# Products of zeros on TensorE during the first load, a different load order, and alternating half groups at the end of a two-layer graph network kernel

## The chip, the cores and the metric

The kernel runs on one NeuronCore of a Trainium2 chip. The metric is the device time of one execution in microseconds (us). TensorE (PE in the profile) multiplies matrices and writes to PSUM; its weight loads (PEld) have a row of their own. VectorE (DVE), ScalarE (ACT) and GpSimd (POOL) do elementwise work and reductions, and SyncE (SP), ACT and POOL issue the DMA transfers.

## The reference

The input x is (16, 1024, 64): 16 batches, 1024 nodes, 64 channels; adj is 1024 x 1024. Two layers follow each other, each with a residual and a layer norm over the channels. Cut to what is computed:

```python
# layer 0
Q, K, V = x @ Wq.T + bq, x @ Wk.T + bk, x @ Wv.T
score = softmax(einsum('bnc,bmc->bnm', Q, K), axis=1)
out   = einsum('bnm,bmc->bnc', score @ adj, V)
x = layernorm(x + out)
# layer 1: both supports are adj
x1 = adj @ x;  x2 = 2 * (adj @ x1) - x
x_cat = [x, x1, x2, x1', x2']      # the second support again, from x and x1
x = layernorm(x + x_cat @ weight + bias)
```

All of it is float32.

## The kernel before, in words

**Layout.** Two batches make a pair, so that a pair's 2 x 64 channels fill the 128 partitions; there are eight pairs (`NP = 8`). The 1024 nodes are eight blocks of 128 (`K8 = 8`). `xs` holds x with the nodes on the partitions, `xT` holds it with the channels on the partitions, and `aT` holds the transposed adj.

**Algebra.** A term that is constant along the softmax axis drops out, so `bq` is not used and the scores are x times `GY`, with `GY = m_w^T xT + gb`. Here `m_w` is the product of the two score weights and `gb` that of one weight with `bk`. Layer 0 forms `U = adj @ x` once, and applies `Wv` after the sum.

**The start (lines 65 to 136).** `wq` and `wk` are 128 x 128 tiles that VectorE sets to zero and whose two diagonal 64 x 64 blocks are loaded: `wq`, `wk` and `bkp` in turn for each half, six transfers in ACT's queue. SP loads x in eight transfers of 512 KB and then aT in eight of 512 KB. GpSimd issues five transfers of weights that are used later, and builds the identity `ident` after them (`make_identity`, lines 84 and 85). `transposed(p)` turns the eight blocks of a pair on TensorE against `ident` into a PSUM tile `pt` (line 104), and ACT copies it to `xT` (line 105). `score_weight` turns `wq` and `wk` (lines 109, 110), VectorE copies them to `wn` (line 111), and `score_weight_2` forms `m_w` and `gb` (lines 115 to 118). `project(p)` makes `GY` of a pair with two products (line 126), and VectorE adds `gb` on the way out of PSUM (line 127). The order is written out by hand:

```python
transposed(0); pm = score_weight(); transposed(1); score_weight_2(pm)
for p in range(NP):
    if p + 2 < NP: transposed(p + 2)
    project(p)
```

PSUM has a pool `ps` of three tiles for all of these, and a pool `pacc` with one tile, `acc`.

**Order of work.** The scheduler is manual: each engine executes in the order in which the program names its instructions. In the profile, one float32 product of 128 columns or more appears as two matmul records; a transpose appears as one.

**Products with adj (`product`).** A 1024 x 1024 product with adj is done by one level of a Strassen-like scheme with seven block products, `p1` to `p7`, instead of eight. `step(name, g, rows)` accumulates one block product of a group `g` (two row blocks of 128 rows; `rows` picks one of them: a half group) into a PSUM tile that a chain of steps shares, in 16 products (8 for a half group), all on line 267. After each step VectorE or ACT takes the state of the tile to the result: line 283 adds it to what is there, line 287 adds it to another tensor. The next step of the same chain accumulates into the same tile, so it waits until that has been read. `p4` is in chain "a", `p3` in chain "b".

**Middle.** For each of 64 (pair, node block) steps the scores are formed, exponentiated and multiplied with `U`; then come the norm of layer 0 and the weights of layer 1. Then there are two more products with adj.

**The end (lines 499 to 543).** `leave(i, c, g, skip, blocks)` is the last layer norm of a group: ACT squares (line 507) and VectorE sums. For a whole group GpSimd takes the inverse root and multiplies. For a half group (`blocks == 1`) it is ACT's square root and VectorE's reciprocal and product (lines 171 to 179 and 513), so that VectorE has four operations, an addition, a sum, a reciprocal and a product, with two of ACT between them. Each block is stored by a transfer of SP. The last four lines of the order are

```python
for g in range(2):
    step("p4", g); leave(1, 0, g)
for i in range(2):
    step("p3", 1, (i,)); leave(0, 1, 1, i, 1)
```

Of the kernel before, what the change touches and what calls it, by code (L numbers as in the profile page):

```python
# [9 lines left out]
FP = mybir.dt.float32  # L10
# [8 lines left out]
def gnn_kernel(  # L19
# [13 lines left out]
    nc = tc.nc  # L33
    ctx.enter_context(tc.manual_schedule())
    N, B, C = out.shape
    P = 128
    K8 = N // P
    NP = B // 2
# [6 lines left out]
    const = ctx.enter_context(tc.tile_pool(name="const", bufs=1))  # L45
# [3 lines left out]
    pacc = ctx.enter_context(tc.tile_pool(name="pacc", bufs=1, space=bass.MemoryType.PSUM))  # L49

    def ps_tile(name):
        return ps.tile([P, 2 * H], FP, tag="ps", name=name)


    xs = big.tile([P, NP, K8, P], FP, tag="xs", name="xs")
    aT = big.tile([P, K8, N], FP, tag="aT", name="aT")
    x_in = x.rearrange("p q k b c -> p q k (b c)")
    a_in = adjT.rearrange("(k p) i -> p k i", p=P)

    def pair_weight(name):  # L60
        w = const.tile([P, P], FP, tag=name, name=name)
        nc.vector.memset(w, 0.0)
        return w

    wq, wk = pair_weight("wq"), pair_weight("wk")
    bkp = const.tile([P, 1], FP, tag="bkp", name="bkp")
    raw = const.tile([P, 5, C], FP, tag="raw", name="raw")
    w1s = const.tile([P, 5, C], FP, tag="w1s", name="w1s")
    for j in range(2):
        s = slice(j * C, (j + 1) * C)  # L70
        nc.scalar.dma_start(wq[s, s], wqT)
        nc.scalar.dma_start(wk[s, s], wkT)
        nc.scalar.dma_start(bkp[s], bk[:, None])
    for p in range(NP):
        nc.sync.dma_start(xs[:, p], x_in[:, p])
    for k in (4, 5, 6, 7, 0, 1, 2, 3):
        nc.sync.dma_start(aT[:, k], a_in[:, k])
    for j in range(2):
        s = slice(j * C, (j + 1) * C)
        nc.gpsimd.dma_start(w1s[s], w1.rearrange("(s c) o -> c s o", c=C))  # L80
        nc.gpsimd.dma_start(raw[s, 3], wvT)
    nc.gpsimd.dma_start(raw[:, 4], b1[None, :].to_broadcast([P, C]))

    ident = const.tile([P, P], FP, tag="ident", name="ident")
    make_identity(nc, ident)
    expo = const.tile([P, G], FP, tag="expo", name="expo")
    nc.vector.memset(expo, -0.5)
    eps = const.tile([P, 1], FP, tag="eps", name="eps")
# [11 lines left out]
    def transposed(p):  # L100

        pt = ps_tile("pt")
        for k in range(K8):
            nc.tensor.transpose(pt[:, ts(k, P)], xs[:, p, k, :], ident)  # L104
        nc.scalar.activation(xT[:, p], pt, AF.Copy)  # L105

    def score_weight():
        pw = ps_tile("pw")
        nc.tensor.transpose(pw[:, 0:P], wq, ident)
        nc.tensor.transpose(pw[:, P : 2 * P], wk, ident)  # L110
        nc.vector.tensor_copy(wn, pw[:, 0 : 2 * P].rearrange("p (a o) -> p a o", a=2))
        return pw

    def score_weight_2(pm):
        nc.tensor.matmul(pm[:, H : H + P], wn[:, 1], wn[:, 0], start=True, stop=True)
        nc.tensor.matmul(pm[:, 2 * H - P : 2 * H - P + 1], wn[:, 0], bkp, start=True, stop=True)
        nc.vector.tensor_copy(m_w, pm[:, H : H + P])
        nc.vector.tensor_copy(gb, pm[:, 2 * H - P : 2 * H - P + 1])
# [4 lines left out]
    def project(p):  # L123
        pg = ps_tile("pg")
        for h in range(2):
            nc.tensor.matmul(pg[:, ts(h, H)], m_w, xT[:, p, ts(h, H)], start=True, stop=True)
        nc.vector.tensor_scalar(GY[:, p], pg, gb, None, op0=ALU.add)

    transposed(0)
    pm = score_weight()  # L130
    transposed(1)
    score_weight_2(pm)
    for p in range(NP):
        if p + 2 < NP:
            transposed(p + 2)
        project(p)


# [17 lines left out]
    for j in range(2):  # L156
        s = slice(j * C, (j + 1) * C)
        nc.vector.tensor_copy(wv[s, s], raw[s, 3])

    def row_sums(sq, g=G):  # L160
        var = small.tile([P, g], FP, tag="var", name="var")
        nc.vector.tensor_reduce(var, sq, AX.X, ALU.add)  # L162
        nc.vector.tensor_scalar(var, var, 1.0 / C, EPS, op0=ALU.mult, op1=ALU.add)  # L163
        return var

    def inverse_root(var, g=G):
        rstd = small.tile([P, g], FP, tag="rstd", name="rstd")
        nc.gpsimd.tensor_tensor(rstd, var, expo[:, 0:g], ALU.pow)  # L168
        return rstd[:, :, None].to_broadcast([P, g, C])

    def inverse_root_2(sq, g):


        var = small.tile([P, g], FP, tag="var", name="var")
        nc.vector.tensor_reduce(var, sq, AX.X, ALU.add)  # L175
        rstd = small.tile([P, g], FP, tag="rstd", name="rstd")
        nc.scalar.activation(rstd, var, AF.Sqrt, bias=eps, scale=1.0 / C)  # L177
        nc.vector.reciprocal(rstd, rstd)
        return rstd[:, :, None].to_broadcast([P, g, C])
# [27 lines left out]
    def by_pair(t):  # L207

        return t.rearrange("p k (q f) -> p q k f", q=NP)
# [190 lines left out]
    step, sums = product(S, xs, by_pair(U), acc_group=1)  # L400
# [53 lines left out]
    def blocked(t):  # L454
        return t.rearrange("p q (k f) -> p q k f", k=K8)

    p = NP - 1
# [4 lines left out]
    step, sums = product(S, blocked(GY), by_pair(Z), xs)  # L462
# [36 lines left out]
    def leave(i, c, g, skip=0, blocks=2):  # L499

        first_block = i * HB + 2 * g + skip
        r = R[:, first_block : first_block + blocks, ts(c, H)].rearrange(
            "p i (b c) -> p i b c", c=C
        )
        nb = B // 2
        sq = att.tile([P, blocks, nb, C], FP, tag="rT", name="sq2")
        nc.scalar.activation(sq, r, AF.Square)  # L507
        rows = sq.rearrange("p i b c -> p (i b) c")
        if blocks == 1:
            engine, rstd = nc.vector, inverse_root_2(rows, nb)  # L510
        else:
            engine, rstd = nc.gpsimd, inverse_root(row_sums(rows))
        engine.tensor_tensor(  # L513
            r, r, rstd.rearrange("p (i b) c -> p i b c", i=blocks), ALU.mult
        )
        for n in range(blocks):
            nc.sync.dma_start(out[ts(first_block + n, P), ts(c, nb)], r[:, n])

    step, sums = product(S, by_pair(Z), by_pair(R), blocked(xT))
# [15 lines left out]
    for g in range(2):  # L535
        step("p7", g)
        leave(1, 1, g)
    for g in range(2):
        step("p4", g)
        leave(1, 0, g)  # L540
    for i in range(2):
        step("p3", 1, (i,))
        leave(0, 1, 1, i, 1)


# [38 lines left out]
```

## Time and profile before

| | |
|---|---|
| time, median of 3 runs | 623.25 us (622.73 to 623.89) |
| profiled execution, span | 621.4 us |
| TensorE matmul busy | 606.1 us, 98% of the span |
| VectorE busy | 335.3 us, 54% |
| ScalarE busy | 225.2 us, 36% |
| GpSimd busy | 86.5 us, 14% |
| DMA | 14.30 MB, mostly in the first 25 us |

TensorE is busy from about 5 us after the start to about 7 us before the end. A row of groups gives the busy time, the mean duration of one instruction, the idle time before them, and what ended most of that. In a timeline, a line is the start in us, the length of the merged stretch in us, the engine, the line of code, the operation, and what ended the idle time before it. Matmul ends are modelled, so that distances between starts say more than lengths[...].

### The profile page before, as it was taken

What the parts mean: (1) busy time and instruction counts of PE and PEld (TensorE: products, weight loads), DVE (VectorE), ACT (ScalarE), POOL (GpSimd) and SP (SyncE); (2) the same over time, 40 slices, a digit from 0 to 9 for tenths busy, and PEclk for the clock granted to TensorE, in tenths of its full rate; (3) what the DMA queues carried; (4) which work ended last, traced back from release to release, by engine and by line L of the source; (5) the groups of instructions that cost most, each with busy time, mean ns of one, the idle gap of its engine ahead of it and who ended that gap; (6) DMA issues with size and microseconds to landing.
All of it is one profiled execution on the core that took longest, in us unless ns stands there. A gap on an engine that the chain in (4) does not pass through costs nothing. (4 is left out here: it accounts for less than half of the span.)

```text
span 621.4 us, 5758 instructions
## 1 busy us (share of the span) xinstructions
PE 606.1 (98%) x2246; PEld 263.1 (42%) x2246; DVE 335.3 (54%) x554; ACT 225.2 (36%) x376; POOL 86.5 (14%) x47
## 2 busy tenths in 40 slices
PE   5999999999999999999999999999999999999994
PEld 4544444433334444343434434344444444444441
DVE  0498212157786767768686776735462332234434
ACT  2300100056656667676666767651100000000011
POOL 2000004400030200303030020300000000140374
PEclk9999999999999999999999999999999999999998
DMA  9600000200000000000000000000000000010012
GB/s 296 264 0 0 1 0 0 68 1 0 2 0 1 1 1 2 1 0 2 0 1 2 0 2 1 0 1 0 1 0 0 1 0 0 1 69 0 34 69 101
DMA packets 5835, 14.30 MB, mean 23 GB/s; under 512 B 1088, under 2 KB 1152, under 8 KB 5808
## 3 DMA queue, kind: packets, MB, share of 16 engines
q1 hardware_dynamic: 5136, 13.63, 5.9%
q0 software_dynamic: 192, 0.23, 0.2%
q8 instruction: 18, 0.29, 0.2%
q10 hardware_dynamic: 480, 0.07, 0.1%
q14 instruction: 9, 0.07, 0.0%
HBM read 9.73 MB, written 4.19 MB: 22 GB/s over the span
## 5 line engine op out<-in xcount | busy, mean ns | idle before, releaser
L313 DVE TENSOR_SCALAR_CACHE_REDUCE e<-sc 128x1024 f32<-128x1024 f32 x128 | 151.6, 1222 | 68.1 <-PE sc L306 68.1
L320 ACT ACTIVATE e<-e,nm 128x1024 f32<-128x1024 f32 x128 | 146.2, 1143 | 74.6 <-DVE e L313 74.5
L306 PE MATMUL sc<-xT,GY 64*128 64x512 f32 x512 | 128.1, 615 | 0.5 <-DVE e L313 0.5
L343 PE MATMUL acc<-e,us 128*64 128x512 f32 x512 | 124.0, 605 | 0.3 <-DVE us L331 0.3
L168 POOL TENSOR_TENSOR rstd<-var,expo 128x16 f32<-128x16 f32 x14 | 40.6, 2903 | 423.5 <-DVE var L163 423.5
L306 PEld LDWEIGHTS sc<-xT,GY 64*128 64x128 f32 x512 | 44.6, 186 | 73.5 <-issue 49.9
L507 ACT ACTIVATE sq<-GY 128x1024 f32<-128x1024 f32 (+1 forms) x9 | 8.7, 962 | 163.1 <-DVE GY L283 151.5
L267 PE MATMUL p<-T,S 128*128 128x512 f32 x144 | 62.8, 592 | 0.0
L343 PEld LDWEIGHTS acc<-e,us 128*64 128x64 f32 x512 | 31.0, 136 | 71.0 <-issue 62.9
L267 PEld LDWEIGHTS p<-T,S 128*128 128x128 f32 x144 | 27.4, 190 | 34.4 <-issue 34.4
L285 ACT ACTIVATE U<-p 128x1024 f32<-128x1024 f32 x6 | 6.2, 1025 | 74.5 <-PE p L267 74.5
L426 POOL TENSOR_TENSOR xs<-xs,mu 128x1024 f32<-128x1024 f32 x8 | 15.0, 1903 | 103.0 <-DVE T L236 92.2
L379 PEld LDWEIGHTS pw<-raw,xT 64*128 64x128 f32 x256 | 21.7, 187 | 17.3 <-issue 7.3
L379 PE MATMUL pw<-raw,xT 64*128 64x192 f32 x256 | 27.1, 332 | 0.0
L104 PE MATMUL pt<-ident,xs 128*128 128x128 f32 x128 | 19.7, 304 | 5.7 <-POOL ident masks.py:199 5.2
L390 DVE TENSOR_TENSOR xT<-pw,raw 128x256 f32<-128x256 f32 x32 | 13.6, 425 | 21.3 <-ACT GY L389 21.3
L105 ACT ACTIVATE xT<-pt 128x1024 f32<-128x1024 f32 x16 | 16.2, 1014 | 21.9 <-PE pt L104 21.9
L320 ACT ACTIVATION_READ_ACCUMULATOR e<-e,nm 128x1 f32 x128 | 24.0, 188 | 0.0
L104 PEld LDWEIGHTS pt<-ident,xs 128*128 128x128 f32 x128 | 16.5, 157 | 14.9 <-issue 9.1
L287 DVE TENSOR_TENSOR GY<-p,xT 128x1024 f32<-128x1024 f32 x7 | 8.6, 1224 | 25.0 <-PE p L267 25.0
L267 PE MATMUL acc<-T,aT 128*128 128x512 f32 x48 | 21.4, 594 | 0.0
L267 PE MATMUL p<-GY,aT 128*128 128x512 f32 x48 | 21.3, 596 | 0.0
(116 smaller groups left out, 604.6 us busy)
## 6 DMA issues: line engine op xcount, KB each, us to landing
xs<-in_x_dram SPq DMA_DIRECT2D x8, 512.0 KB, 6.5
aT<-in_adjT_dram SPq DMA_DIRECT2D x8, 512.0 KB, 10.2
out_dram<-GY SPq DMA_DIRECT2D x16, 256.0 KB, 2.3
aT<-in_adjT_dram SPq DMA_DIRECT2D x1, 1024.0 KB, 6.0
w1s<-in_w_dram POOLq DMA_DIRECT2D x2, 80.0 KB, 4.9
wq<-in_wqT_dram ACTq DMA_DIRECT2D x2, 16.0 KB, 4.1
wk<-in_wkT_dram ACTq DMA_DIRECT2D x2, 16.0 KB, 4.7
raw<-in_wvT_dram POOLq DMA_DIRECT2D x2, 16.0 KB, 4.6
```

The costliest lines, as they stand in the source:

```text
L104: nc.tensor.transpose(pt[:, ts(k, P)], xs[:, p, k, :], ident)
L105: nc.scalar.activation(xT[:, p], pt, AF.Copy)
L168: nc.gpsimd.tensor_tensor(rstd, var, expo[:, 0:g], ALU.pow)
L267: nc.tensor.matmul(pt[:, ts(i, H)], left_of(k, 2 * g + i), right_of(k), start=(start and k == 0), stop=(k == HB - 1), skip_group_check=not ...
L306: nc.tensor.matmul(sc[j][:, ts(h, H)], GY[s, p, ts(m, P)], xT[s, p, ts(h, H)], start=True, stop=True,)
L313: nc.vector.tensor_scalar(E[n][:, j], sc[j], -1.0, None, op0=ALU.mult, op1=ALU.min, accum_out=NM[n][:, j : j + 1],)
L320: nc.scalar.activation(E[n][:, j], E[n][:, j], AF.Exp, bias=NM[n][:, j : j + 1], scale=-1.0, accum_out=SM[n][:, j : j + 1],)
L343: nc.tensor.matmul(ACC[p][j * C : (j + 1) * C, ts(h, H)], us[:, j], es[:, j, ts(h, H)], start=(m == 0), stop=(m == K8 - 1),)
L379: nc.tensor.matmul(pw[:, j, ts(k, 3 * C)], xT[s, p, ts(2 * c + k, P)], raw[s, 0:3].rearrange("p w c -> p (w c)"), start=True, stop=True,)
L390: nc.vector.tensor_tensor(at(xT), to[:, 0], raw[:, 4:5, None].to_broadcast([P, 2, 2, C]), ALU.add)
L426: nc.gpsimd.tensor_tensor(rows_of(p), rows_of(p), mu[:, p, :, None].to_broadcast([P, G, C]), ALU.subtract)
L507: nc.scalar.activation(sq, r, AF.Square)
```

## The change

It has three parts. First, TensorE gets products of a zero tile `still` that nobody reads (`idle_turns(n)`, into the `acc` tile of the pool `pacc`): six before the first transposes, three after them, and two after the transposes of the score weights. They are meant to keep TensorE at work while x is loaded. The order of the start changes with them: one more pair is transposed before the first `project`. Second, the identity is built before GpSimd's transfers, `wk` is loaded from GpSimd's queue ahead of the others, `wq` is first in ACT's queue with both halves, `bkp` comes behind it, and the first pair of x is loaded in two halves. Third, the last group of `p4` is done in half groups that alternate with those of `p3`, so that two half groups of one PSUM tile do not follow each other directly.

```diff
+    still = const.tile([P, P], FP, tag="still", name="still")
+    nc.vector.memset(still, 0.0)
+    ident = const.tile([P, P], FP, tag="ident", name="ident")
+    make_identity(nc, ident)
     wq, wk = pair_weight("wq"), pair_weight("wk")
...
-    for j in range(2):
-        s = slice(j * C, (j + 1) * C)
+    halves = [slice(j * C, (j + 1) * C) for j in range(2)]
+    for s in halves:
         nc.scalar.dma_start(wq[s, s], wqT)
-        nc.scalar.dma_start(wk[s, s], wkT)
+        nc.gpsimd.dma_start(wk[s, s], wkT)
+    for s in halves:
         nc.scalar.dma_start(bkp[s], bk[:, None])
-    for p in range(NP):
+    for k in range(0, K8, 4):
+        nc.sync.dma_start(xs[:, 0, k : k + 4], x_in[:, 0, k : k + 4])
+    for p in range(1, NP):
         nc.sync.dma_start(xs[:, p], x_in[:, p])
...
-    ident = const.tile([P, P], FP, tag="ident", name="ident")
-    make_identity(nc, ident)
...
+    def idle_turns(n):
+
+        pt = pacc.tile([P, N], FP, tag="acc", name="idle")
+        for _ in range(n):
+            nc.tensor.matmul(pt[:, 0:P], still, still, start=True, stop=True)
+
+    idle_turns(6)
     transposed(0)
+    idle_turns(3)
+    transposed(1)
     pm = score_weight()
-    transposed(1)
+    idle_turns(2)
+    transposed(2)
     score_weight_2(pm)
     for p in range(NP):
-        if p + 2 < NP:
-            transposed(p + 2)
+        if p + 3 < NP:
+            transposed(p + 3)
         project(p)
...
-    for g in range(2):
-        step("p4", g)
-        leave(1, 0, g)
+    step("p4", 0)
+    leave(1, 0, 0)
     for i in range(2):
-        step("p3", 1, (i,))
-        leave(0, 1, 1, i, 1)
+        for name, q in (("p4", (1, 0)), ("p3", (0, 1))):
+            step(name, 1, (i,))
+            leave(*q, 1, i, 1)
```

More of the change, by code (lines that the diff above doesn't have):

```diff
@@ L77, in gnn_kernel @@
         nc.sync.dma_start(aT[:, k], a_in[:, k])
-    for j in range(2):
-        s = slice(j * C, (j + 1) * C)
+    for s in halves:
         nc.gpsimd.dma_start(w1s[s], w1.rearrange("(s c) o -> c s o", c=C))
```

## The prediction

> **What bounds the kernel now.** I read the busy time by stages first. I cut the stages at the first matmul (5.20), at the first pair of products that start at half the former distance (15.90), at the first product with adj (32.97) and at the last whole group (599.20).
>
> ```profile
> core 0: us, PE busy (x) PEld busy (x) DVE busy (x) ACT busy (x) POOL busy (x), PEclk, DMA share, GB/s
> 0.00:5.20 5.20, 0.00 (x0) 0.00 (x0) 0.34 (x4) 0.35 (x1) 4.01 (x11) 1.00 0.65 220
> 5.20:15.90 10.70, 9.58 (x33) 7.34 (x34) 0.78 (x3) 4.01 (x4) 0.00 (x0) 1.00 1.04 338
> 15.90:32.97 17.07, 17.07 (x70) 9.66 (x69) 8.98 (x7) 5.12 (x5) 0.00 (x0) 1.00 0.58 231
> 32.97:599.20 566.23, 565.50 (x2114) 240.47 (x2113) 315.51 (x526) 211.72 (x361) 70.70 (x31) 1.00 0.02 6
> 599.20:621.40 22.20, 13.98 (x32) 5.63 (x31) 9.68 (x14) 3.97 (x6) 11.80 (x6) 0.90 0.25 95
> ```
>
> From 32.97 to 599.20 TensorE has 0.73 us without work. So a us saved ahead of 32.97 is a us of the total, as long as nothing else there is tied to absolute time. The rest lies in the two ends. The start on TensorE, from the timeline:
>
> ```profile
> 5.21 1.97 PE L104 MATMUL pt<-ident,xs 128*128 128x128 f32 x8 [5.21 <-POOL ident masks.py:199]
> 7.69 0.45 PE L109 MATMUL pw<-ident,wq 128*128 128x128 f32 x1 [0.52 <-DMA wq<-in_wqT_dram]
> 10.06 0.64 PE L115 MATMUL pw<-wn 128*128 128x128 f32 x2
> 10.80 0.56 PE L116 MATMUL pw<-bkp,wn 128*128 128x1 f32 x2
> 11.85 1.94 PE L104 MATMUL pt<-ident,xs 128*128 128x128 f32 x8 [0.49 <-PE pw L116]
> 13.58 3.17 PE L126 MATMUL pg<-xT,m_w 128*128 128x512 f32 x4
> 16.59 1.04 PE L104 MATMUL pt<-ident,xs 128*128 128x128 f32 x8
> 17.46 1.88 PE L126 MATMUL pg<-xT,m_w 128*128 128x512 f32 x4
> ```
>
> Nothing runs on TensorE until the identity is there at 5.2, behind GpSimd's five transfers. Then it is slow: eight transposes take 1.97 us up to the line at 11.85 and 1.04 us from 16.59 on. Starts lie 0.21 us apart early (5.47, 5.68, 5.90), 0.107 us later; records of 512 columns 0.86 and 0.43. The change of pace falls between 15.3 and 16.1. PEclk reads 1.00 all along, so that column does not show it. Now the end, from the chain of waits:
>
> ```profile
> 599.18 6.88 PE p L267 x16
> ...
> 606.08 1.24 DVE GY L287
> ...
> 609.99 0.60 DVE GY L283
> 610.59 0.04 issue
> 610.63 3.71 PE p L267 x8
> 614.35 0.02 issue
> 614.37 0.70 DVE GY L283
> ...
> 617.24 0.69 DVE GY L513
> ```
>
> The first half group of `p3` ends at 609.48 (599.18 + 6.87 + 3.43), the second begins at 610.63: it waits until VectorE has read the shared tile, and VectorE was still busy with the norm of `p4`'s second group. After the last product come 3.56 us of norm (614.37 to 617.93) and the store.
>
> [...] here it took 10.7 us from the first transpose. In that time TensorE had gaps at 7.2 to 7.7, about 10.6 and 11.4 to 11.85; from 11.85 on it ran without a gap for 4 us, and then the pace changed. [...] ACT issued its six at 1.04, 1.63, 2.26, 2.91, 3.56 and 4.20.
>
> **The change part by part.**
>
> *Identity and weights.* Identity: memset 0.24 and select 0.29, 0.6 us with the gap. Ahead of the transfers it is ready at 1.4 instead of 5.2. `wk`: GpSimd issues take 0.58 us, so the second half goes out at about 2.1 and, by the landing of the like-sized `raw` from the same queue (median 4.6), is there at 6.7. `wq`'s second half moves from 2.91 to about 1.75; with its slower landing (4.6) it is there by 6.4. `bkp`'s second half moves from 4.20 to about 2.95. It landed after 6.5 us, at 10.7, which is just what the line at 10.80 shows; the first half took 4.9. So it comes at 7.9 to 9.5. The later weights come up to 2.5 us later, but are first used at 34.38: nothing.
>
> *x.* The third x transfer was issued at 4.37, when the first had landed; so x0 is there at 4.35. Half of it, at the rates of 303 to 408 GB/s seen between 2.5 and 4.0, about 0.65 us earlier: 3.6 to 3.7. The other pairs follow at 1.3 us each (512 KB at 410 GB/s) and are early from then on. aT's last transfer landed at 25.3 and is needed by VectorE's sums after 30: hidden.
>
> *Zero products.* One of 128 columns is two records of 0.214 us at slow pace (line 115: 10.06 and 10.27). The zero tile is the first memset of VectorE (0.84, 0.17 long), so TensorE starts at about 1.1. Records up to the transposes of pair 3: zeros 12, pair 0 8, zeros 6, pair 1 8, weights 2, zeros 4, pair 2 8, `m_w` 2 and `gb` 2 short ones: 52 x 0.214 = 11.1 us if all were slow, to 12.2. The six zeros end at 3.7, as the first half of x0 lands; the second half is needed at 4.5, pair 1 at 6.7. So TensorE has no gap from 1.1[...]. With a release at w, what is left halves: 12.2 - (12.2 - w)/2, or 8.4 to 10.1 with the middle at 9.2. The landing of `bkp` allows 8.2 to 9.8. I take 9.6 for the start of pair 3's transposes.
>
> From there: five pairs of transposes and products at 2.59 us (16.59 to 19.18) and three products at 1.715 make 12.95 + 5.15 = 18.1; the products with adj begin at 27.7 instead of 32.97. **Head: 5.3 us saved.** ACT's copy (1.02) and VectorE's addition (1.28) fit in 2.59 as they did. VectorE's sums for `p5` follow its last addition and move along. The three `idle` tiles are in a pool that is first used again far later.
>
> *The end.* The second half of `p4` and the halves of `p3` now alternate between two tiles. TensorE waits for nothing after 599.18 + 4 x 3.43 = 612.9, 1.45 us before the old 614.35. But VectorE has four half-group norms in a row, each 3.56 us from the addition to the product, with the next addition queued behind the product, although it waits for ACT for most of that. TensorE needs 3.43. VectorE can begin when the sum of the whole group is done, 602.95 plus 0.1; 603.05 + 4 x 3.56 = 617.3 against 617.93. So most of TensorE's 1.45 us is lost to this queue. GpSimd's last inverse root and product fall away; they ended at 615.2 and were not last. If the handovers add 0.1 each, 617.7. **End: 0.6 us saved** (0.2 to 1.0).
>
> Sum: 5.3 + 0.6 = 5.9 us; 623.25 - 5.9 = 617.35, say 617.4.
>
> **The rivals.**
>
> *A. The faster pace comes late, at about 11,* because [...] the wait for x leaves a gap. [...] Against: the slow stage of before shows gaps enough to explain itself. Pair 3 starts at 12.2 - 0.6 = 11.6: head 3.3, total 3.9, 619.4.
>
> *B. An operand takes the place of the identity:* `bkp` or `wk` lands as late as `bkp` did, 10.7, since [...] x is now fed more densely. For: a DMA share near 1 in the slow stage. Against: the issue is 1.2 us earlier. Pair 3 at 11.1: head 3.8, total 4.4, 618.9.
>
> *C. Neither zeros nor transposes count* and the release stays at 15.9. Then pair 3 starts at 12.2, its transposes end at 13.9 and the first product at 16.6 (2.0 of its 3.43 us slow, the rest at twice the pace); four pairs at 2.59 and three products give 32.1. Head 0.8, total 1.4: 621.9.
>
> *D. Slower.* The 22 zero records are 4.7 us of TensorE at slow pace. If they release nothing and the start moves only from 5.2 to 1.1, they cost 0.6 net; if the four norms take 4.0 us each beside GpSimd's and DMA's traffic, the end is at 619.05, 1.1 later. 623.25 + 1.7 = 625.0. Against: the queued zeros end before x lands by the numbers above, and GpSimd's product overlapping VectorE in the last stage stretched by only 0.26 us (2.16 against 1.90) and VectorE's by 0.01.
>
> **How the numbers follow.** Forecast 0.72, A 0.10, B 0.10, C 0.05, D 0.03. The predicted time is the forecast's. Its own width, [...] (8.4 to 10.1 at pair 3, so 617.4 + 0.5 or - 1.2) and the end, gives 616.2 to 618.3; A and B reach to 619.4. The range 616.4 to 619.7 takes in the most of these and leaves out C, D and the tails, some 2 in 10 at most. The bound of 0.2% is 1.25 us: forecast, A and B are faster, C (1.4) is about at the bound and I split it. Faster 0.94, same 0.03, slower 0.03.
>
> **What would show it.** In the new profile: the first matmul near 1.1 on the zero tile; no gap of TensorE over 0.3 us before pair 3; starts 0.107 us apart from 4.5 to 8 on; pair 3's transposes at 8.4 to 10.1; the first product with adj near 27.7; in the last stage no wait of TensorE for VectorE, and VectorE's four norms end to end. It is wrong if starts stay 0.21 us apart beyond 9, if TensorE waits for `bkp` or `wk` beyond 9.8, if a wait appears between 33 and 599 that was not there, or if the last product on VectorE comes over 5 us after TensorE's last.

## The result, and the profile after

| | before | after |
|---|---|---|
| time, median (6 runs each) | 623.29 us (622.73 to 623.89) | 620.69 us (619.64 to 622.22) |
| profiled execution, span | 621.4 us | 619.1 us |
| first product with adj | 32.97 us | 31.64 us |
| from there to VectorE's last product's start | 584.27 us | 583.33 us |

The ratio is 0.9959, with a 95% interval of 0.9945 to 0.9972: 2.6 us faster, 1.7 to 3.4. The forecast was 5.9 us (617.4, range 616.4 to 619.7). A ratio and its interval are worked out apart and need not be the quotient of two medians.

First the busy time by stages of the kernel after. I cut where the clock changes; the seventh number after the span, PEclk, now shows it.

```profile
core 0: us, PE busy (x) PEld busy (x) DVE busy (x) ACT busy (x) POOL busy (x), PEclk, DMA share, GB/s
...
1.05:5.33 4.28, 4.28 (x20) 4.26 (x21) 0.26 (x4) 1.28 (x1) 4.00 (x8) 1.00 0.72 235
5.33:8.74 3.41, 0.92 (x8) 0.73 (x6) 0.00 (x0) 1.02 (x1) 0.56 (x1) 1.00 0.65 215
8.74:12.16 3.42, 2.88 (x14) 2.88 (x15) 0.43 (x1) 0.87 (x1) 0.00 (x0) 0.50 0.99 317
12.16:31.64 19.48, 19.48 (x87) 11.63 (x87) 9.34 (x9) 6.29 (x7) 0.00 (x0) 1.00 0.76 302
31.64:597.88 566.24, 565.52 (x2114) 240.48 (x2113) 315.56 (x526) 211.65 (x361) 70.67 (x31) 1.00 0.02 6
```

The middle is untouched: 566.24 us against 566.23. Until 5.33 TensorE ran at half pace, with the starts of zeros and transposes 0.21 us apart (the first stage's 1.00 only means that no change is on record yet), to 8.74 at full pace (0.11 us apart), until 12.16 at half (0.21), and from there at full pace (0.11). The clock's last change is at 616.32, and in the kernel before it changed at 16.16 and 616.91. In the one trace these changes lie 3.413, 3.413 and 604.159 us apart, in the other 600.746: 1, 1, 177 and 176 times 3.413 us. A stretch of that length, counted off from a change, is called a window below; counted back to the start, the windows of the 17 traces begin at 0.17 to 3.31 us. In the stage from 5.33 to 8.74 TensorE has 0.92 us of work in 3.41. The timeline of TensorE says why:

```profile
1.05 2.93 PE L137 MATMUL idle<-still 128*128 128x128 f32 x12 [1.05 <-DVE still L66]
3.78 1.80 PE L108 MATMUL pt<-ident,xs 128*128 128x128 f32 x8
5.42 0.83 PE L137 MATMUL idle<-still 128*128 128x128 f32 x6
9.28 1.97 PE L108 MATMUL pt<-ident,xs 128*128 128x128 f32 x8 [3.03 <-DMA xs<-in_x_dram]
...
13.49 1.07 PE L108 MATMUL pt<-ident,xs 128*128 128x128 f32 x8
14.40 1.88 PE L130 MATMUL pg<-xT,m_w 128*128 128x512 f32 x4
```

The zeros begin at 1.05 and the first transposes at 3.78, as forecast. Then TensorE waits 3.03 us for the second pair of x, finds half the clock when that is there (eight transposes 1.97 us long, against 1.07 at 13.49), and reaches pair 3 at 13.49, not at 9.6. The transfer that it waited for, issued at 1.65, in the view of its line:

```profile
L82 SPq DMA_DIRECT2D xs<-in_x_dram x1: 424/424/424, 1.7 to 1.7; - x1
...
DMA to landing us min/median/max: 7.6/7.6/7.6
```

It landed at 9.2. In the kernel before, the same pair, issued at 1.18, landed at 5.9. And `bkp`, in the view of its tile:

```profile
L78 ACTq DMA_DIRECT2D bkp<-in_bk_dram x2: 617/618/618, 2.4 to 3.0; - x2
DMA to landing us min/median/max: 7.0/8.2/9.3
```

Its halves were issued at 2.39 and 3.04, the second 1.2 us earlier than before, and landed at 9.4 and 12.3: 9.3 us for the second, against 6.5 before.

The end, from the chain of waits:

```profile
597.88 1.24 DVE GY L301
...
601.79 0.60 DVE GY L301
...
605.25 0.61 DVE GY L297
...
608.72 0.61 DVE GY L301
...
612.20 0.61 DVE GY L297
...
614.97 0.69 DVE GY L527
```

TensorE is not in this chain any more. VectorE's four half-group norms stand end to end, 3.47 us apart.

### The profile page after: what moved, and what is told of

Its sections match the earlier page's. It is cut to its first block, busy times and chain, and to the rows that moved or that the text cites. A ratio compares the mean times of both kernels' runs of the same rounds, so it can differ in the third digit from the quotient of the medians.

```text
span 619.1 us, 5817 instructions
## 1 busy us (share of the span) xinstructions
PE 606.8 (98%) x2268; PEld 265.7 (43%) x2268; DVE 337.2 (54%) x560; ACT 225.9 (36%) x379; POOL 82.7 (13%) x47
## 5 line engine op out<-in xcount | busy, mean ns | idle before, releaser
L182 POOL TENSOR_TENSOR rstd<-var,expo 128x16 f32<-128x16 f32 x13 | 37.7, 2902 | 421.5 <-DVE var L177 421.5
L281 PEld LDWEIGHTS p<-T,S 128*128 128x128 f32 x144 | 27.4, 190 | 34.4 <-issue 34.4
L109 ACT ACTIVATE xT<-pt 128x1024 f32<-128x1024 f32 x16 | 16.2, 1013 | 20.0 <-PE pt L108 20.0
L281 PE MATMUL p<-T,aT 128*128 128x512 f32 x48 | 21.3, 592 | 0.0
L281 PE MATMUL acc<-T,S 128*128 128x512 f32 x48 | 21.1, 592 | 0.0
## 6 DMA issues: line engine op xcount, KB each, us to landing
aT<-in_adjT_dram SPq DMA_DIRECT2D x8, 512.0 KB, 10.1
```

Of the source, the lines that this page charges most:

```text
L281: nc.tensor.matmul(pt[:, ts(i, H)], left_of(k, 2 * g + i), right_of(k), start=(start and k == 0), stop=(k == HB - 1), skip_group_check=not ...
```

## The experiments

Times are in us; landings and starts are those of the profiled execution. Pair 1 is the second pair of x, pair 3 the fourth. "Waits" is what TensorE waited for transfers in the start, in total; in the two kernels without zeros it contains the wait for the first half of x (3.6 and 3.4 us), and it is left blank where the identity comes late. Each ratio is to the kernel before on the same chip, whose medians are 623.05 to 623.46 us.

| kernel | pair 1 lands | `bkp` lands | waits | pair 3 starts | first product with adj | median | ratio (95%) |
|---|---|---|---|---|---|---|---|
| before | 5.9 | 10.7 | | | 32.97 | 623.29 | |
| after | 9.2 | 12.3 | 3.0 | 13.49 | 31.64 | 620.69 | 0.9959 (0.9945 to 0.9972) |
| after again | 6.7 | 11.9 | 3.2 | 12.75 | 30.89 | 620.42 | 0.9962 (0.9947 to 0.9977) |
| end alone | 6.0 | 11.5 | | | 31.53 | 622.26 | 0.9985 (0.9972 to 0.9998) |
| no zeros | 7.0 | 10.5 | 5.1 | 11.98 | 30.61 | 620.09 | 0.9954 (0.9939 to 0.9969) |
| wk with ACT | 8.1 | 10.2 | 1.5 | 11.45 | 29.59 | 620.22 | 0.9962 (0.9945 to 0.9979) |
| later weights with SP | 6.7 | 10.5 | 1.9 | 10.89 | 29.04 | 618.65 | 0.9927 (0.9913 to 0.9941) |
| nothing with GpSimd | 6.5 | 8.5 | 0.8 | 10.54 | 28.68 | 619.02 | 0.9942 (0.9921 to 0.9964) |
| more zeros | 8.1 | 12.4 | 0 | 13.01 | 31.16 | 620.24 | 0.9967 (0.9955 to 0.9979) |
| one queue | 7.9 | 10.3 | 1.2 | 11.48 | 29.62 | 619.08 | 0.9954 (0.9936 to 0.9972) |
| one queue, no zeros | 8.1 | 10.4 | 6.2 | 13.08 | 31.23 | 621.07 | 0.9983 (0.9969 to 0.9997) |
| old loads | 5.7 | 10.0 | 1.8 | 11.26 | 29.40 | 619.19 | 0.9946 (0.9925 to 0.9966) |
| x unsplit | 5.5 | 12.8 | 3.5 | 13.35 | 34.34 | 622.56 | 0.9977 (0.9963 to 0.9991) |
| x unsplit, weights with SP | 5.8 | 10.2 | 0.6 | 11.64 | 29.78 | 618.05 | 0.9916 (0.9902 to 0.9930) |
| x unsplit, bkp first | 6.8 | 7.8 | 4.2 | 14.45 | 32.59 | 621.99 | 0.9987 (0.9976 to 0.9997) |
| the same, weights with SP | 6.6 | 7.7 | 3.0 | 11.94 | 30.09 | 619.34 | 0.9942 (0.9929 to 0.9955) |
| x unsplit, nothing with GpSimd | 5.8 | 8.0 | 1.7 | 11.08 | 29.22 | 619.18 | 0.9938 (0.9918 to 0.9958) |

Three things to know in reading it. The profiled execution is not always a middle one: with wk in ACT's queue it took 618.82 us where the median is 620.22, with x unsplit 623.66 where it is 622.56. The ratio can part from the medians: with one queue they give 0.9930, the ratio is 0.9954.

And the executions of one kernel differ by what the clock did. Each has its mean granted clock on record, and one stretch of 3.41 us at half lowers that by about 0.003 (the changed kernel's two traces, with one such stretch and with none, have 0.995 and 0.998). With the old loads, six executions at 0.996 to 0.998 took 617.6 to 619.2 us and five at 0.992 to 0.995 took 621.2 to 623.3. With x unsplit, six at 0.996 or more took 619.9 to 621.0 and eleven at 0.995 or less 621.3 to 624.4. Where the later weights went to SP and `wk` stayed with GpSimd, all 17 executions of the three kernels have 0.996 or more. So a median also says how often the clock was taken back.

**The end alone.**

```diff
 # the kernel before, with the change's last lines
-    for g in range(2):
-        step("p4", g)
-        leave(1, 0, g)
+    step("p4", 0)
+    leave(1, 0, 0)
     for i in range(2):
-        step("p3", 1, (i,))
-        leave(0, 1, 1, i, 1)
+        for name, q in (("p4", (1, 0)), ("p3", (0, 1))):
+            step(name, 1, (i,))
+            leave(*q, 1, i, 1)
```

> The kernel before with the third part of the change alone (halves of p4 and p3 alternating). Theory (the ends add up; VectorE's four half-group norms in a row set the end): the start stays as before, first product with adj at 33.0 us, TensorE has no wait after the last whole group, and the time from the first product with adj to the end shrinks by 0.9 us as in the changed kernel: 622.4 us, 0.7 to 1.1 below the kernel before. Rival (the change's gain is the start's alone): 623.3.

The ratio is 0.9985, 0.9 us (0.1 to 1.7). In the traces, from the first product with adj to the start of VectorE's last product it is 583.30 us here (31.53 to 614.83), 583.33 in the kernel after and 584.27 before: 0.95 us, the theory's number. That the ratio gives the same is in part chance, as its interval is wide and the start varies: the first product with adj stands at 31.53 with the very start of the kernel before, not at 33.0. The timeline of TensorE:

```profile
11.65 0.35 PE L116 MATMUL pw<-bkp,wn 128*128 128x1 f32 x2 [1.06 <-DMA bkp<-in_bk_dram]
12.50 1.07 PE L104 MATMUL pt<-ident,xs 128*128 128x128 f32 x8 [0.49 <-PE pw L116]
```

`bkp` is waited for until 11.65 here, later than the 10.80 of before, and still the transposes at 12.50 are fast (1.07 us), where those at 11.85 were slow (1.94): by the clock's record it was released at 10.7 in this execution, at 16.2 in that one. The same start can differ by 1.4 us between two executions.

**The changed kernel again.** No edit.

> The changed kernel again, unaltered, for a second trace on the same chip as the others. Theory (two things vary between executions and set the start: the phase of the clock's windows, and the landing of [...] the second pair of x): that pair lands somewhere between 7 and 9.5 us, the clock is taken back for 3.4 us only if the gap before it fills most of a window, the first product with adj begins at 29.5 to 31.7, and from there to VectorE's last product it is 584.0 us as in all kernels with the new end. Rival (the first trace is typical to 0.2 us): landing at 9.3, clock taken back, 31.6.

Pair 1 landed at 6.7 this time, a little earlier than the theory had it, the clock was not taken back (1.00 through windows with 2.16 and 1.90 us of work), and the start came at 30.89, within the theory's range. The waits of TensorE up to there:

```profile
PE pw L120 <- DMA bkp<-in_bk_dram: 1.5, 1, 1.5
PE idle L137 <- DVE still L66: 1.1, 1, 1.1
PE pt L108 <- DMA xs<-in_x_dram: 0.9, 2, 0.5
PE pw L114 <- DMA wk<-in_wkT_dram: 0.8, 1, 0.8
```

With pair 1 less late, `bkp` (11.9), `wk` (8.5) and pair 3 (12.6) are what TensorE waits for: 3.2 us. Pair 3 started at 12.75; 3.2 us earlier is the 9.6 of the forecast.

**No zeros.**

```diff
-    idle_turns(6)
     transposed(0)
-    idle_turns(3)
     transposed(1)
     pm = score_weight()
-    idle_turns(2)
     transposed(2)
```

> The changed kernel without its 22 records of zero products (11 products that nobody reads; nothing of the result is left out). Theory (the zeros release the clock early, but the wait for the second pair of x gives most of it back): the clock stays at half until a window of 3.4 us is filled after the second pair lands, that is until 12.7 to 16.1; pair 3's transposes start at about 14 and run slow: 0.5 to 2.6 us above the changed kernel, 621.2 to 623.3. Rival (the zeros do nothing, since the transposes alone release the clock): equal to the changed kernel or up to 0.4 us below it, 620.3 to 620.7.

0.9954 against 0.9959 and 0.9962: the rival's number. In the changed kernel the zeros bring nothing that can be measured. The rival's mechanism is not what the trace shows, though. The clock came as late as the theory had it, at 13.0 and not at 5.3:

```profile
11.98 1.55 PE L108 MATMUL pt<-ident,xs 128*128 128x128 f32 x8
...
15.09 1.04 PE L108 MATMUL pt<-ident,xs 128*128 128x128 f32 x8
```

Even so pair 3 started at 11.98, before the 13.49 and 12.75 of the changed kernel. There `bkp` came at 12.3 and 11.9, here at 10.5; whether that is due to the missing zeros or to chance is not shown.

**More zeros.** `idle_turns(3)` becomes `idle_turns(18)`.

> The changed kernel with 18 zero products instead of 3 between the first and the second pair of x (15 more, 3.2 us at full pace; nothing of the result changes). Theory (the gap lets the clock be taken back, which costs half of 3.4 us where it happens): no clock is taken back, and the time is up to 1.5 us below the changed kernel's, 619.0 to 620.5, with less spread; where the second pair lands early the extra zeros cost up to 2 us. Rival (the gap costs only its own length): equal or up to 1 us slower, 620.5 to 621.7.

The clock was not taken back, as the theory has it (the windows from 7.00 to 17.24 are at 1.00 and filled with work), but the transposes of pair 1 began at 10.23 behind the zeros, 2.1 us after that pair had landed. The ratio, 0.9967, is that of the changed kernel. What the bridge saves in clock it spends in its own length.

**wk with ACT.**

```diff
-        nc.gpsimd.dma_start(wk[s, s], wkT)
+        nc.scalar.dma_start(wk[s, s], wkT)
```

> The changed kernel with wk back in ACT's queue (wq and wk in turn, then bkp); the five later transfers of weights stay with GpSimd and go out at 1.6 us. Theory (any traffic of GpSimd's queue in the first microseconds[...]): the second pair of x still lands late, at 8 to 9.5, TensorE has a gap of 2 to 3 us, and the time is within 0.7 us of the changed kernel, 620.0 to 621.4. Rival (it is wk's transfers in particular): the second pair lands by 6.5, no gap, 617 to 618.5.

Pair 1 at 8.1, and 0.9962: as the theory said, though the gap was 1.3 us and not 2 to 3. `wk` is not the cause by itself.

**Later weights with SP.**

```diff
     for s in halves:
-        nc.gpsimd.dma_start(w1s[s], w1.rearrange("(s c) o -> c s o", c=C))
-        nc.gpsimd.dma_start(raw[s, 3], wvT)
-    nc.gpsimd.dma_start(raw[:, 4], b1[None, :].to_broadcast([P, C]))
+        nc.sync.dma_start(w1s[s], w1.rearrange("(s c) o -> c s o", c=C))
+        nc.sync.dma_start(raw[s, 3], wvT)
+    nc.sync.dma_start(raw[:, 4], b1[None, :].to_broadcast([P, C]))
```

> The changed kernel with the five later transfers of weights (w1s, raw) moved from GpSimd's queue to SP's, behind aT; wk stays with GpSimd. Theory (GpSimd's traffic delays x): the second pair of x lands by 6.7 instead of 9.3, TensorE has no gap over 0.5 us, the clock is not taken back, the first product with adj begins at 27.5 to 28.7 instead of 31.6: 617.0 to 618.3 us. Rival (x is late because its own transfers are issued without a pause and in two halves, whatever GpSimd does): the second pair lands at 8.5 or later, 620 to 621.

0.9927, with an interval that lies below those of the changed kernel in both its measurements: 2.0 us gained by moving five transfers that the kernel before first uses at 34.4. Pair 1 landed at 6.7 and `bkp` at 10.5. The start, 29.04, and the time fall short of the theory's 28.7 and 618.3, for TensorE still waited 1.1 us for pair 1, 0.5 for `bkp` and 0.3 for `wk`.

**Nothing with GpSimd.** Both edits together.

> The changed kernel with wk in ACT's queue and the later weights behind aT in SP's: nothing in GpSimd's queue. Theory B: three transfers of x and six small ones are still in flight together, so the second pair lands at 6 to 7.5; bkp, last of six in ACT's queue, at 9 to 11; first product with adj at 28.3 to 29.5, 617.9 to 619.1 us. Rival (GpSimd's queue is the whole cause): second pair by 6.0, bkp by 9, 617 to 617.9.

Pair 1 at 6.5 and the first product with adj at 28.68, theory B's numbers, and the earliest start of all; `bkp` came at 8.5, sooner than theory B had it. Its median, 619.02, is no better than the last kernel's, and its runs spread more: four took 617.7 to 619.5, and two, with a granted clock of 0.995 or less, 621.3 and 621.4.

**One queue.**

```diff
+    for p in (1, 2):
+        nc.sync.dma_start(xs[:, p], x_in[:, p])
     for s in halves:
-        nc.scalar.dma_start(wq[s, s], wqT)
-        nc.gpsimd.dma_start(wk[s, s], wkT)
+        nc.sync.dma_start(wq[s, s], wqT)
+        nc.sync.dma_start(wk[s, s], wkT)
     for s in halves:
-        nc.scalar.dma_start(bkp[s], bk[:, None])
+        nc.sync.dma_start(bkp[s], bk[:, None])
...
-    for p in range(1, NP):
+    for p in range(3, NP):
         nc.sync.dma_start(xs[:, p], x_in[:, p])
...
     transposed(1)
+    transposed(2)
     pm = score_weight()
     idle_turns(2)
-    transposed(2)
```

The later weights stand behind aT, as above.

> The changed kernel with all loads of the start in SP's queue, in the order of their use: the first pair in two halves, pairs 1 and 2, wq and wk, bkp, pairs 3 to 7, aT, the later weights; on TensorE the third pair is transposed before the score weights. Theory (small transfers in other queues[...] are what delays x and bkp; in one queue they are short): the second pair lands by 6, bkp by 8, TensorE has no gap over 0.5 us, the first product with adj begins at 26.5 to 27.7: 616.0 to 617.3 us. Rival (x is late because of its own many transfers in flight): the second pair lands at 7 or later, 618.5 to 620.5.

The rival won on the landing: pair 1 at 7.9, with no other queue in use. So other queues are not the whole cause. The time, 619.08, is the rival's too.

**One queue, no zeros.**

> The kernel with one queue without the 22 records of zero products. Theory (with x in time the zeros are worth what the clock gains by them): the clock is released 3.4 to 6.8 us after the first transposes at 3.7, so at 7.1 to 10.5, pair 3's transposes start at 9 to 10, 0.3 to 1.5 us slower than with the zeros. Rival (zeros release nothing that the transposes don't): equal within 0.2 us or faster.

The start moves from 29.62 to 31.23 and the ratio from 0.9954 to 0.9983, 1.8 us, where the intervals just touch: here the zeros are worth something, more than the theory had, as pair 1 landed at 8.1 and the clock came at 11.8. The timeline shows one more thing:

```profile
8.18 3.68 PE L110 MATMUL pt<-ident,xs 128*128 128x128 f32 x16 [2.88 <-DMA xs<-in_x_dram]
11.65 0.34 PE L115 MATMUL pw<-ident,wq 128*128 128x128 f32 x1
...
13.08 1.07 PE L110 MATMUL pt<-ident,xs 128*128 128x128 f32 x8
```

From 8.18 to 11.78 TensorE did nothing but float32 transposes, 16 of x and one of `wq`, at slow pace (0.22 us each), and the window from 8.37 to 11.78 was busy for all of its 3.41 us. Then the pace was full: eight took 1.07 us at 13.08. So in this trace transposes alone released the clock.

**Old loads.**

```diff
-    halves = [slice(j * C, (j + 1) * C) for j in range(2)]
-    for s in halves:
+    for j in range(2):
+        s = slice(j * C, (j + 1) * C)
         nc.scalar.dma_start(wq[s, s], wqT)
-        nc.gpsimd.dma_start(wk[s, s], wkT)
-    for s in halves:
+        nc.scalar.dma_start(wk[s, s], wkT)
         nc.scalar.dma_start(bkp[s], bk[:, None])
-    for k in range(0, K8, 4):
-        nc.sync.dma_start(xs[:, 0, k : k + 4], x_in[:, 0, k : k + 4])
-    for p in range(1, NP):
+    for p in range(NP):
         nc.sync.dma_start(xs[:, p], x_in[:, p])
```

> The changed kernel with the loads of the kernel before, in its queues and order (x in whole pairs, wq, wk and bkp in turn in ACT's queue), and only the identity still ahead of GpSimd's transfers. [...] Theory (the second pair is late because the changed kernel puts four transfers of x and the small ones into flight together): the second pair lands at 5.7 to 6.2 as before, TensorE has a gap of at most 0.7 us there, the clock is not taken back; but the third pair lands at 10.3 and bkp at 10.7, so pair 3's transposes start at 11.4 to 12 and the first product with adj at 29.5 to 30.2: 618.8 to 620.0 us. Rival (the second pair is late because TensorE and the identity start earlier, not because of the loads): it lands at 7 or later and the time is the changed kernel's, 620.2 to 620.9.

Pair 1 at 5.7 and 0.9946: as the theory said, and not slower than the changed kernel. The second part of the change, without the identity, brought nothing that can be measured.

**x unsplit.**

```diff
-    for k in range(0, K8, 4):
-        nc.sync.dma_start(xs[:, 0, k : k + 4], x_in[:, 0, k : k + 4])
-    for p in range(1, NP):
+    for p in range(NP):
         nc.sync.dma_start(xs[:, p], x_in[:, p])
```

> The changed kernel with the first pair of x in one transfer instead of two halves; nothing else. Theory A (the 2 KB pieces of the halves are what slows the stream): the second pair lands by 6.0, and the time falls by 1 to 2 us. Theory B (it is the number of transfers in flight and the small ones among them): the second pair still lands at 6.6 to 9.3, the first transposes start at 4.35 instead of 3.7, and the time is within 0.8 us of the changed kernel's.

Theory A was right on pair 1 (5.5) and wrong on the time: the median rose, and the ratio's interval overlaps the changed kernel's. The timeline of TensorE:

```profile
12.93 0.56 PE L118 MATMUL pw<-bkp,wn 128*128 128x1 f32 x2 [3.23 <-DMA bkp<-in_bk_dram]
13.35 1.95 PE L106 MATMUL pt<-ident,xs 128*128 128x128 f32 x8
```

`bkp` landed at 12.8, TensorE waited 3.23 us, and the clock was taken back for two windows, from 12.33 to 19.15 (the transposes at 13.35 are slow, 1.95 us for eight), behind a window with 0.78 us of work. Mending one late operand laid bare the next. The six of its 17 executions that kept the clock took 619.9 to 621.0, much like the changed kernel.

**x unsplit, later weights with SP.** Both edits.

> The changed kernel with the first pair of x in one transfer and the later weights behind aT in SP's queue; wk stays with GpSimd. If theory A holds, the second pair lands by 6.0 and the time is 617 to 618. If theory B holds, it is within 0.6 us of the kernel that moved the later weights alone (618.65): 618.2 to 619.3.

0.9916, 5.2 us (4.4 to 6.1) below the kernel before: the lowest median of all, better than the changed kernel beyond both intervals, and about the gain that was forecast for that one. Pair 1 landed at 5.8, as theory A has it. Its shortest execution, 617.8, is no shorter than those of three others (617.6 with the old loads, 617.7 with nothing in GpSimd's queue, 617.6 with that and x unsplit); what sets it apart is that none of its six lost the clock. Its timeline, from the slowest of its six executions:

```profile
4.62 1.94 PE L106 MATMUL pt<-ident,xs 128*128 128x128 f32 x8 [0.64 <-DMA xs<-in_x_dram]
...
7.64 1.91 PE L106 MATMUL pt<-ident,xs 128*128 128x128 f32 x8
...
10.40 1.04 PE L106 MATMUL pt<-ident,xs 128*128 128x128 f32 x8
```

After 4.62 TensorE waits for no transfer. What is left here is the clock: the window with the gap of 0.64 us had 2.78 us of work and no release at its end, the next one had 3.41 and the release at 10.14.

**x unsplit, bkp first; and the same with the later weights with SP.** To the edit of x this is added:

```diff
     for s in halves:
+        nc.scalar.dma_start(bkp[s], bk[:, None])
+    for s in halves:
         nc.scalar.dma_start(wq[s, s], wqT)
         nc.gpsimd.dma_start(wk[s, s], wkT)
-    for s in halves:
-        nc.scalar.dma_start(bkp[s], bk[:, None])
```

> The changed kernel with the first pair of x in one transfer and bkp ahead of wq in ACT's queue; everything else stays, GpSimd's transfers too. Theory (in the changed kernel two operands stand where the identity stood: the second pair of x, late because the first was loaded in halves, and bkp, late at 10.5 to 12.8 [...]): the second pair lands by 6.0, bkp at 7 to 10, TensorE does not wait for bkp, the clock is not taken back, and the first product with adj begins at 28.0 to 29.5: 617.3 to 618.8 us. Rival (whichever small transfer is last in its queue comes at 10 to 12, now wq): TensorE waits for wq until 9 or later instead, 619.5 to 621.

> The same with the later weights behind aT in SP's queue. Theory: no operand is later than TensorE by more than 0.5 us, pair 3's transposes start at 9.3 to 10.3, the first product with adj begins at 27.4 to 28.4, which is the start that was predicted for the changed kernel: 616.7 to 617.8 us. Rival (the start is bound by TensorE's and the clock's own course, not by operands): no faster than the kernel with the later weights moved and x unsplit, 618.0.

The rival won in the first, and its time was even longer than that one's: `bkp` landed at 7.8, and now `wq`, last in that queue, came at 10.9. TensorE's timeline and, below it, the busy time by stages of the same kernel:

```profile
11.00 0.45 PE L111 MATMUL pw<-ident,wq 128*128 128x128 f32 x1 [3.09 <-DMA wq<-in_wqT_dram]
```

```profile
3.91:7.32 3.41, 2.32 (x20) 2.08 (x20) 0.00 (x0) 1.65 (x2) 1.98 (x4) 1.00 0.72 209
7.32:10.74 3.42, 0.58 (x6) 0.34 (x4) 0.00 (x0) 1.02 (x1) 0.00 (x0) 1.00 1.06 310
10.74:14.15 3.41, 3.15 (x15) 3.19 (x16) 0.42 (x1) 0.00 (x0) 0.00 (x0) 0.50 1.03 338
```

A stretch with 0.58 us of work in 3.42 at full clock, and the next at half. In the second kernel `wq` came at 9.9, and it missed its forecast too: the operands were not early, so it did not answer the question that it was built for. Pair 1 landed at 6.8 and 6.6 although x was not split.

**x unsplit, nothing with GpSimd.**

> The changed kernel with the first pair of x in one transfer, wk in ACT's queue, and the later weights behind aT in SP's queue (nothing in GpSimd's). Theory: the second pair lands by 6.0, the third[...] at 8.5 to 9.3, bkp at 8.5 to 9.5; pair 3's transposes start at 10 to 10.6, first product with adj at 28.1 to 28.7: 617.4 to 618.1 us. Rival (the halves of the first pair are harmless and the second pair's early landing without GpSimd's queue is all there is): equal to the same kernel with halves, 619.0.

Pair 1 at 5.8 and `bkp` at 8.0, but TensorE waited 1.1 us for pair 3 (landed at 11.0). The first product with adj is at 29.22 and the ratio 0.9938: against 0.9942 with halves the time cannot tell them apart.

## Why the prediction was wrong

**The identity and the zeros: right.** TensorE began at 1.05 (forecast 1.1), transposes at 3.78 (3.7), and the clock was released at 5.33 (4.5 to 8). That it would come so early was my estimate; the trace of the kernel before, with its release at 16.16, did not show it.

**The step that failed is the landing of the operands,** in two sentences: "The other pairs follow at 1.3 us each (512 KB at 410 GB/s) and are early from then on", and, on `bkp`, "So it comes at 7.9 to 9.5". Pair 1 came at 9.2 and 6.7 in two executions, where it was needed at 6.3 and 6.2, and `bkp` at 12.3 and 11.9. The rate was not 410 GB/s there: the changed kernel's trace has 271 between 4 and 6 us and 199 between 6 and 8. The kernel before could have told me, for its trace has 330 and 189 in these stretches. Its third pair landed at 10.3, 4.4 us behind the second, and only the later ones came 1.3 apart, so I laid the rate of a later stretch on the first 9 us. And I kept the landing times of a profile in which SP had issued two transfers of x until 4.37 for one in which it had issued four by 2.12.

**What the runs show of the cause.** For `bkp` behind `wq` in ACT's queue it goes with GpSimd's queue. With all seven transfers there, `bkp` landed at 11.9 to 12.8 (10.5 once); with the five later weights, at 10.0 to 11.5; with the two of `wk`, at 10.2 and 10.5; with none, at 8.5 and 8.0. Two pairs of kernels differ in nothing but `wk`'s queue: from GpSimd's to ACT's, `bkp` went from 10.5 to 8.5 with halves, and from 10.2 to 8.0 without. What the denser feed adds to the landings the forecast put at nothing; only rival B had it. For pair 1, all six traces with x whole and `bkp` not ahead have it at 5.5 to 6.0, and all nine with halves at 6.5 to 9.2, but also the two with x whole and `bkp` ahead at 6.6 and 6.8. So it was late where the first pair was cut or `bkp` went first, and not where a half of `wq` did (1.04 against 1.18 in the kernel before). By what means is open. It was not that the DMA engines together were full: between 6 and 8 us their busy share, the number before the last, is 1.02 in the kernel before (first line) and 0.59 in the kernel after:

```profile
6.00:8.00 2.00, 1.49 (x7) 0.95 (x5) 0.00 (x0) 0.93 (x2) 0.00 (x0) 1.00 1.02 189
6.00:8.00 2.00, 0.25 (x3) 0.06 (x1) 0.00 (x0) 0.64 (x1) 0.00 (x0) 1.00 0.59 199
```

The traces of the two kernels have 16 records of each transfer's landing. Of pair 1's, 14 had come at 6.8 in the changed kernel's trace, the 15th at 7.4 and the last at 9.2; in the kernel before all 16 came between 5.3 and 5.9. So some 2.4 of the 3.0 us that TensorE waited went on the last two. And the kernel with `bkp` ahead of `wq` only passed the delay on: with the old order `bkp` was last in ACT's queue and came at 12.8, with the new one `wq`, at 10.9.

**What followed from it.** The wait of 3.03 us left a window with 0.92 us of work, and the next 3.42 us ran at half clock, in which 2.88 us of work are worth half: 1.4 us. 13.49 - 3.03 - 1.44 = 9.0, inside the 8.4 to 10.1 that TensorE's own part was forecast to take. The same sum holds where the clock stayed: 12.75 - 3.2 = 9.6 in the second trace, 10.89 - 1.9 = 9.0 with the weights moved, 10.54 - 0.8 = 9.7 with nothing at GpSimd, 11.26 - 1.8 = 9.5 with the old loads. So in these traces the count of records and the clock's part were right, and the operands are the miss. With x unsplit and the later weights moved the sum does not hold: 11.64 - 0.6 = 11.0, as the window with the gap of 0.64 us before the first transposes released nothing and the clock came at 10.1. All this is a subtraction over traces; no kernel had all operands early at once.

**The rivals.** B (an operand takes the place of the identity) named the mechanism: it had `bkp` at 10.7 and 618.9 us. It was given 0.10, it did not name pair 1 of x (A's gap by a wait for x comes nearest), and its size was too small, for `bkp` landed later than in the kernel before and, as in A, a late clock came on top in the first trace. I should have asked what faster engines set off: transfers that were hidden behind the identity now stood in the open.

**The zeros: a size.** Their 22 records were the part of the change that the forecast leaned on most. In the changed kernel they bring nothing (0.9954 without them), in the kernel with one queue 1.8 us. They did release the clock early (5.3 against 13.0 without them); but late operands set the start, and a faster TensorE only waited longer for them.

**The end: right, and a bit better.** 0.95 us instead of 0.6. The mis-sized term is the distance of VectorE's norms: 3.47 us and not 3.56, since the next addition begins 0.08 before the last product's recorded end. From the first product with adj TensorE's last product ends 1.4 us earlier than before (at 611.6, against 614.3), VectorE's 0.95 (at 615.66). So about a third of what TensorE saved is lost to VectorE's queue, and not most of it, as the prediction said.

## What to carry to other kernels

When a wait at a kernel's start is removed, list each operand behind it with its landing, and ask how the landing moves when the queues run together; a landing time read from a profile in which the bottleneck spaced the transfers is not one to keep. Transfers that are needed late should not be issued in the first microseconds: moving five of them behind the large loads was worth 2.0 us here, about what the change gained at the start (1.3 and 2.1 us in its two traces). Of work that only keeps the clock up, ask whether TensorE's own pace sets the time: it brought 1.8 us with one queue and nothing in the changed kernel, whose start was set by late operands.

## What the runs showed that I had not expected

- In the kernel with one queue and no zeros, a window of 3.41 us that was busy throughout with float32 transposes, and with nothing else, released the clock (at 11.78). Rival C had transposes count for nothing.
- The clock was taken back after windows of 3.41 us with 0.58, 0.78 and 0.92 us of work, and kept after one with 1.68 us. In the 17 traces, with the windows counted off in steps of 3.41 us from the changes on record, every window that released it had 2.83 us of work or more, and none that did not had more than 2.81, but for one with 2.90 in the kernel before.
- Two executions with the same start differ by 1.4 us in its length (32.97 and 31.53), with the clock's release at 16.2 and at 10.7. A single trace of a start is worth no more than that.
- The second half of `bkp`, 64 values of 4 bytes, took 9.3 us to land beside x and GpSimd's transfers, longer than 512 KB of x issued before it (7.6).
